# The chunk state of a state-space layer, held as 64x384 or as 128x192

## The chip, the cores and the metric

The kernel runs on one core of a Trainium2 chip. The metric is the device time of one execution in microseconds (us), the median of several runs. All data and all matrix products are in 32-bit floats.

## The reference

The kernel computes two residual layers on images of 64x64 positions with 192 channels, 8 of them. The change lies in layer 0, in its state-space part. For each image the 4096 positions are one sequence; a projection and a causal convolution give `x` (6 heads of 64 columns, 384 in all), `B` and `C` (64 columns each, shared by the heads), and a step `dt` for each head. With `A` negative for each head, the part that matters is:

```python
dA_cs = jnp.cumsum(dt * A, axis=2)                       # within a chunk
scores = einsum('bcin,bcjn->bcij', Cm, Bm)[..., None] * exp(seg) * dt   # masked: j <= i
y = einsum('bcijh,bcjhp->bcihp', scores, x)              # inside a chunk
decay_last = exp(dA_cs[:, :, -1:, :] - dA_cs)
states = einsum('bcjn,bcjh,bcjhp->bchnp', Bm, dt * decay_last, x)
chunk_decay = exp(dA_cs[:, :, -1, :])
new = carry * chunk_decay + states                       # from chunk to chunk
y = y + einsum('bcin,bchnp,bcih->bcihp', Cm, prev, exp(dA_cs))
```

So a chunk has a **state** of 64 numbers (`n`) for each of 384 columns (6 heads of 64). The **update** decays the state by one factor for each head and adds a product of the chunk's `B` and weighted `x`. The **readout** multiplies the state before the chunk with the chunk's `C` and scales each row by a factor for each head. The kernel works with chunks of 128 positions, which gives the same result as the reference's 256.

## The kernel before

**Stages.** `tile_kernel` runs `layer0` over all 8 images, and then `layer1`, which is four times as long and has nothing to do with the change. `layer0` cuts each image into 8 tiles of 512 positions (64 tiles, numbered `T`), and each tile into 4 chunks of 128 (256 chunks, numbered `c` within a tile).

**Order of the work.** `layer0` is written as 18 generators, among them `convolve`, `steps_in_time`, `scores`, `turn`, `states`, `mixer` and `output`. Each yields steps, and a step names an engine and a cost in us. A planner (`Flow`) plays these steps through as the program is built: it always issues the step that can start first by the written costs, with a small bonus from the generator's rank, and `keep` pins the order so found for each engine. On the chip each engine runs its queue in this order, and an instruction that has to wait holds up all behind it. `take` and `give` count the free buffers of a kind in the plan; `wait` waits for a mark that another generator sets.

**Buffers.** PSUM, which TensorE (PE) writes, has eight banks. Five have the tag `mm` and serve the wide products. Three have the tag `sm`, and everything that belongs to a chunk shares them: `p_g` (the product of `B` and `C`), `p_t` (the chunk's `x`, turned), `p_b` (its `B`, turned), `p_i` (readout), `p_n` (update), `p_y` (result inside the chunk), `p_u` (result turned back), and once a tile `p_c` (cumulative sums). `xdt`, `xw` and `t1` have one buffer each.

**Around the change.** `convolve` (L478 on) leaves `B` and `C` of a tile in one tile `cvb` of 128 partitions, 64 each, and two ACT instructions (L529, L530) put them through SiLU into `bm` and `cm`, each on partitions 0 to 63. `turn` turns `x` and `B` of a chunk (L715, L731); VectorE (DVE) makes of `p_t` the two weighted forms `xdt` (L721) and `xw` (L726). `dec` (L618) holds for each tile the factors for each chunk and head, in three planes: plane 1 is the factor of a row for the readout, plane 2 that of the whole chunk, the same on all 128 partitions. `states` then goes through the chunks:

- the readout: PE multiplies `cm` with the state `st`, both on 64 partitions, into `p_i` (L756), and DVE scales it into `t1` (L758); the first chunk of an image has none
- the update: PE multiplies `bt` and `xw` into 64 partitions of `p_n` (L767); DVE decays the old state (L777) and adds `p_n` (L780), both on 64 partitions by 384 columns. The first chunk of an image is a copy (L772).

`mixer` makes `p_y` from `e` and `xdt` (L803, L806), and DVE adds `t1` to it (L819). It holds its bank while it waits for `t1`.

On PE a product of f32 is issued as two passes, each with a weight load of its own (PEld), so that 256 products show as 512 matmuls.

Of the kernel before, what the change touches and what calls it, by code (L numbers as in the profile page):

```python
# [205 lines left out]
def layer0(tc, consts, x, x1s, mv1, w_in, w_out, w_fc1, w_fc2, rows):  # L206
# [12 lines left out]
    with ExitStack() as ctx:  # L219
# [260 lines left out]
        def convolve():  # L480

            for T, (b, t) in enumerate(tiles):
                yield "wait", ("cin", T, 0)
                cin = got["cin", T]
                yield "take", "cv"
                cv = got["cv", T] = tp.tile([128, 3, TT], F32, name="cv", bufs=2)
                cb = tp.tile([128, TT], F32, name="cvb")
                bm = got["bm", T] = tp.tile([NS, TT], F32, name="bm", bufs=2)
                cm = got["cm", T] = tp.tile([NS, TT], F32, name="cm", bufs=2)
                dst = [cv[:, 0], cv[:, 1], cv[:, 2], cb]  # L490
                done = [0.0] * 4
                for pair in ((0, 1), (2, 3)):
                    for mt in pair:
                        yield "wait", ("cin", T, mt)
                        done[mt] = yield step(
                            "ACT",
                            0.81,
                            lambda: [
                                nc.scalar.activation(
                                    dst[mt],  # L500
                                    cin[:, mt, 0:TT],
                                    AF.Identity,
                                    bias=v128["c1b"][:, mt : mt + 1],
                                    scale=c1w[:, mt, 0:1],
                                )
                            ],
                        )
                    for k in range(1, 4):
                        for mt in pair:
                            done[mt] = yield step(  # L510
                                "DVE",
                                0.77,
                                lambda: [
                                    nc.vector.scalar_tensor_tensor(
                                        dst[mt],
                                        cin[:, mt, k : k + TT],
                                        c1w[:, mt, k : k + 1],
                                        dst[mt],
                                        ALU.mult,
                                        ALU.add,  # L520
                                    )
                                ],
                                done[mt],
                            )
                cin_done(T, max(done))
                if t == NT - 1:
                    cin_done(T, max(done))
                yield step("ACT", 1.5, lambda: [nc.scalar.activation(cv, cv, AF.Silu)], max(done), "silu")
                yield step("ACT", 0.62, lambda: [nc.scalar.activation(bm, cb[0:64], AF.Silu)], None, "silu")  # L529
                f.at["cv", T] = yield step("ACT", 0.62, lambda: [nc.scalar.activation(cm, cb[64:128], AF.Silu)], None, "silu")  # L530

        def gate():
# [144 lines left out]
        def scores():  # L677

            for T in range(len(tiles)):
                yield "wait", ("cv", T)  # L680
                bm, cm = got["bm", T], got["cm", T]
                for c in range(NQ):
                    tk = slice(c * Q, c * Q + Q)
                    yield "take", "sm"
                    pg = qp.tile([128, DIN], F32, name="p_g", tag="sm")
                    q = yield step(
                        "PE",
                        0.26,
                        lambda: [nc.tensor.matmul(pg[:, :Q], bm[:, tk], cm[:, tk], start=True, stop=True)],
                        f.at["cv", T],  # L690
                    )
                    gm = ch.tile([128, Q], F32, name="gm")
                    q = yield step("DVE", 0.28, lambda: [nc.vector.tensor_mul(gm, pg[:, :Q], up)], q)
                    f.give("sm", q)
                    yield "wait", ("p", T, c)
                    e = got["e", T, c]
                    f.at["e", T, c] = yield step(
                        "DVE", 1.02, lambda: [nc.vector.tensor_mul(e, e, bc(gm, 1, [128, NH, Q]))]
                    )

        def turn():

            for T in range(len(tiles)):
                yield "wait", ("w2", T)
                yield "wait", ("cv", T)
                dt, w2, cv, bm = got["dt", T], got["w2", T], got["cv", T], got["bm", T]
                for c in range(NQ):
                    tk = slice(c * Q, c * Q + Q)
                    yield "take", "sm"
                    px = qp.tile([128, DIN], F32, name="p_t", tag="sm")  # L710
                    r = yield step(
                        "PE",
                        0.4,
                        lambda: [
                            nc.tensor.transpose(px[:, i * 128 : i * 128 + 128], cv[:, i, tk], ident) for i in range(3)  # L715
                        ],
                    )
                    yield "take", "xdt"
                    xdt = got["xdt", T, c] = ch.tile([128, DIN], F32, name="xdt", bufs=1)
                    f.at["xdt", T, c] = yield step(  # L720
                        "DVE", 0.55, lambda: [nc.vector.tensor_mul(hv(xdt), hv(px), bc(dt[:, c], 2, heads))], r  # L721
                    )
                    yield "take", "xw"
                    xw = got["xw", T, c] = ch.tile([128, DIN], F32, name="xw", bufs=1)
                    r = yield step(
                        "DVE", 0.55, lambda: [nc.vector.tensor_mul(hv(xw), hv(px), bc(w2[:, c], 2, heads))], r  # L726
                    )
                    f.give("sm", r)
                    yield "take", "sm"
                    pb = qp.tile([128, DIN], F32, name="p_b", tag="sm")  # L730
                    q = yield step("PE", 0.2, lambda: [nc.tensor.transpose(pb[:, :NS], bm[:, tk], ident[:NS, :NS])], 0.0)  # L731
                    f.fork(keep_b(T, c, pb, q, r))

        def keep_b(T, c, pb, q, r):
# [5 lines left out]
        def states():  # L740

            st = None
            for T, (b, t) in enumerate(tiles):
                yield "wait", ("w2", T)
                yield "wait", ("cv", T)
                dec, cm = got["dec", T], got["cm", T]
                if t == 0:
                    st = None
                for c in range(NQ):
                    tk = slice(c * Q, c * Q + Q)  # L750
                    if st is not None:
                        yield "take", "t1"
                        t1 = got["t1", T, c] = ch.tile([128, DIN], F32, name="t1", bufs=1)
                        yield "take", "sm"
                        pi = qp.tile([128, DIN], F32, name="p_i", tag="sm")
                        q = yield step("PE", 0.7, lambda: [nc.tensor.matmul(pi, cm[:, tk], st, start=True, stop=True)])  # L756
                        q = yield step(
                            "DVE", 0.55, lambda: [nc.vector.tensor_mul(hv(t1), hv(pi), bc(dec[:, 1, c], 2, heads))]  # L758
                        )
                        f.give("sm", q)  # L760
                        f.at["t1", T, c] = q
                    yield "wait", ("xw", T, c)
                    bt, xw = got.pop(("bt", T, c)), got.pop(("xw", T, c))
                    yield "take", "sm"
                    pn = qp.tile([128, DIN], F32, name="p_n", tag="sm")
                    q = yield step(
                        "PE", 0.7, lambda: [nc.tensor.matmul(pn[:NS], bt, xw, start=True, stop=True)], f.at["xw", T, c]  # L767
                    )
                    f.give("xw", q)
                    new = sp.tile([NS, DIN], F32, name="st")  # L770
                    if st is None:
                        q = yield step("DVE", 0.5, lambda: [nc.vector.tensor_copy(new, pn[:NS])], q)  # L772
                    else:
                        yield step(
                            "DVE",
                            0.6,
                            lambda: [nc.vector.tensor_mul(hv(new), hv(st), bc(dec[:NS, 2, c], 2, [NS, NH, HD]))],  # L777
                            0.0,
                        )
                        q = yield step("DVE", 0.55, lambda: [nc.vector.tensor_add(new, new, pn[:NS])], q)  # L780
                    f.give("sm", q)
                    st = new
                f.at["states", T] = q
# [1298 lines left out]
```

## Time and profile before

| what | us |
|---|---|
| median of 3 runs (lowest, highest) | 22789.71 (22783.53, 22798.81) |
| the profiled execution, its own time | 22798.87 |
| its span, first to last instruction | 22797.2 |
| PE busy over the span | 21475.4 (94%) |
| DVE busy | 21149.8 (93%) |
| ACT busy | 19859.8 (87%) |
| POOL busy | 16101.6 (71%) |
| stretch of layer 0 (100 to 4660 us of the span): PE, DVE, ACT, POOL busy | 4247.9, 3745.9, 3016.1, 611.5 |

The profile is of one execution. A busy time is the time in which an engine had an instruction under way; PE's is not PE at its peak, since matmuls are pipelined and their ends are modelled. A group of instructions is named by its line in the kernel, its engine and operation, and the tiles that it writes and reads; "idle before" is the time that the engine stood still just ahead of such instructions, with what ended it.

### The profile page before, as it was taken

The numbers are of one execution on the slowest core, as the hardware profiler recorded it, in microseconds if no ns is written. First come the engines' busy times: TensorE is split into PE (matmuls) and PEld (weight loads), VectorE is DVE, ScalarE is ACT, GpSimd is POOL, SyncE is SP. The second block draws the span as 40 slices with busy tenths as digits, with TensorE's granted clock in tenths as the row PEclk, the third lists the DMA queues.
The fourth block names the chain that finished last, engine by engine and source line by source line (L and its number), as shares of the span: only waits on it lengthen the run. The fifth ranks groups of instructions, "written<-read, shape, count | busy, mean of one in ns | idle before, by whom it ended". The sixth has DMA issues, their size and how long they took to land. (4 is left out here: it accounts for less than half of the span.)

```text
span 22797.2 us, 348200 instructions
## 1 busy us (share of the span) xinstructions
PE 21475.4 (94%) x118788; PEld 10903.6 (48%) x118788; DVE 21149.8 (93%) x22445; ACT 19859.8 (87%) x35227; POOL 16101.6 (71%) x12872
## 2 busy tenths in 40 slices
PE   8999999979999999999999999999999999999999
PEld 4444444435554555455545554554455445544554
DVE  7888888869999999999989998999899999999998
ACT  5666666759998999899989998999899989988998
POOL 1111111129995999599959995999599969987997
PEclk8999999989999999999999999999999999999999
DMA  2111111123333333333333333333333333333332
GB/s 53 44 42 46 46 44 46 41 85 93 93 93 109 91 94 94 110 92 93 93 109 93 93 91 110 92 95 92 110 93 94 89 114 93 93 84 116 93 94 78
DMA packets 1706714, 1954.31 MB, mean 86 GB/s; under 512 B 538112, under 2 KB 1039776, under 8 KB 1695712
## 3 DMA queue, kind: packets, MB, share of 16 engines
q1 hardware_dynamic: 1704928, 1932.03, 31.2%
q8 instruction: 933, 15.29, 0.3%
q14 instruction: 853, 6.99, 0.1%
HBM read 1316.16 MB, written 212.60 MB: 67 GB/s over the span
## 5 line engine op out<-in xcount | busy, mean ns | idle before, releaser
L1805 POOL TENSOR_TENSOR hs<-hs,cb 128x1024 f32<-128x1024 f32 x6144 | 14578.3, 2373 | 497.2 <-POOL cy L1803 4.0
L1791 DVE TENSOR_TENSOR_SCAN hs<-ea,cy,g 128x512 f32<-128x512 f32 x10752 | 12922.4, 1269 | 185.8 <-PE g L1775 170.1
L1749 ACT ACTIVATE ea<-dr,an 128x512 f32<-128x512 f32 x12288 | 8141.0, 710 | 454.7 <-DVE hs L1791 414.8
L1740 ACT ACTIVATE pw<-duT,bt 128x384 f32<-128x384 f32 x14304 | 7817.3, 601 | 19.4 <-DMA xo<-xt 19.4
L1820 PE MATMUL y<-hs,sel 128*64 128x512 f32 x24576 | 6629.7, 618 | 357.5 <-POOL hs L1805 337.3
L1775 PE MATMUL g<-ident,pw 128*128 128x128 f32 x43008 | 6101.0, 281 | 63.7 <-DVE hs L1791 15.5
L1775 PEld LDWEIGHTS g<-ident,pw 128*128 128x128 f32 x43008 | 4615.8, 141 | 2550.0 <-issue 1235.9
L1763 PEld LDWEIGHTS g<-dg,duT 128*64 128x64 f32 x24576 | 1556.6, 136 | 2067.5 <-issue 1497.9
L1803 POOL COPY cy<-hs 128x2 f32<-128x2 f32 x6144 | 1152.1, 188 | 1921.3 <-DVE hs L1791 1887.5
L1763 PE MATMUL g<-dg,duT 128*64 128x128 f32 x24576 | 2257.5, 282 | 182.0 <-DVE hs L1791 106.2
L1820 PEld LDWEIGHTS y<-hs,sel 128*64 128x64 f32 x24576 | 1234.0, 135 | 1560.2 <-issue 869.9
L1791 DVE TENSOR_TENSOR_SCAN hs<-ea,g 128x512 f32<-128x512 f32 x1536 | 1754.4, 1205 | 156.0 <-PE g L1775 122.0
L382 POOL TENSOR_TENSOR s<-xs 96x512 f32<-96x512 f32 x64 | 121.7, 1901 | 2138.7 <-DVE xs L360 1849.4
L1259 DVE SCALAR_TENSOR_TENSOR xs<-pad,p,xs 128x2048 f32<-128x2048 f32 x384 | 899.9, 2351 | 133.6 <-ACT xs L1243 123.7
L1654 PE MATMUL p_dt<-xdbl,wd 13*128 13x512 f32 x1536 | 869.7, 647 | 97.2 <-DVE duT L1683 71.5
L382 POOL TENSOR_TENSOR s<-sq 96x512 f32<-96x512 f32 x128 | 182.1, 1423 | 934.1 <-ACT sq L395 829.9
L1619 PE MATMUL p_d<-xc,wx 128*44 128x512 f32 x1536 | 797.0, 603 | 25.1 <-DMA xc<-xo 25.1
L972 PE MATMUL p_f<-h,wf 96*128 96x512 f32 x1536 | 756.5, 631 | 43.8 <-ACT zs L567 27.4
L360 DVE SCALAR_TENSOR_TENSOR x<-xx,p,x 96x512 f32<-96x512 f32 x1024 | 782.8, 814 | 15.2 <-ACT x L349 15.0
L360 DVE SCALAR_TENSOR_TENSOR xs<-xin,p,xs 96x512 f32<-96x512 f32 x1024 | 747.5, 771 | 3.7 <-ACT xs L349 3.7
L992 PE MATMUL p_f<-m,wf 128*96 128x512 f32 x1536 | 692.7, 601 | 0.0
L1676 PEld LDWEIGHTS p_du<-ident,de 128*128 128x128 f32 x3072 | 323.7, 141 | 617.7 <-DVE de L1667 407.1
(214 smaller groups left out, 19356.8 us busy)
## 6 DMA issues: line engine op xcount, KB each, us to landing
cb<-cd SPq DMA_DIRECT2D x4096, 128.0 KB
dr<-de SPq DMA_DIRECT2D x3072, 128.0 KB
xc<-xo SPq DMA_DIRECT2D x256, 768.0 KB
dg<-dz SPq DMA_DIRECT2D x256, 512.0 KB
e<-csd SPq DMA_DIRECT2D x256, 384.0 KB
ut<-xo SPq DMA_DIRECT2D x128, 768.0 KB
ut<-xo SPq DMA_DIRECT2D x256, 384.0 KB
xo<-xs SPq DMA_DIRECT2D x48, 1024.0 KB
```

The source lines that it names most:

```text
L360: nc.vector.scalar_tensor_tensor(im(out[:, ct]), tap(ct, j), w[:, ct, j : j + 1], im(out[:, ct]), ALU.mult, ALU.add)
L1259: nc.vector.scalar_tensor_tensor(xs, tap(d, h, j), kw[:, d, j : j + 1], xs, ALU.mult, ALU.add)
L1619: nc.tensor.matmul(st["p_d"][:44], wx[:, d, k], st["xc"][:, d], start=d == 0, stop=d == DT - 1)
L1654: nc.tensor.matmul(ps, st["wd"][32:45, d * 128 : d * 128 + 128], xds[s % 2][32:45], start=True, stop=True)
L1740: o(nc.scalar.activation(to, what, AF.Copy, scale=by))
L1749: nc.scalar.activation(ea[:, f], state[s]["dr", d][:, f], AF.Exp, scale=an[:, k, p, at : at + 1])
L1763: nc.tensor.matmul(gs[f][i * 64 : i * 64 + 64, j * 128 : j * 128 + 128], state[s]["duT"][:, j, (2 * d + f) * 64 : (2 * d + f) * 64 + 64], ...
L1775: nc.tensor.transpose(gs[f][:, j * 128 : j * 128 + 128], state[s]["pw", p, j][:, 2 * d + f].rearrange("p a b -> p (a b)"), ident,)
L1791: nc.vector.tensor_tensor_scan(rev(h[:, f]), rev(ea[:, f]), rev(g[f]), 0.0 if first(s) else state[s - 1]["cy"][:, p, d, f : f + 1], ALU.mu ...
L1803: o(nc.gpsimd.tensor_copy(st["cy"][:, p, d], h[:, :, last]))
L1805: o(nc.gpsimd.tensor_mul(h, h, bc(st["cb", p], 1, [128, 2, TT])))
L1820: o(nc.tensor.matmul(y[half[f]], sel, hc[:, f], start=p == ORDER[0] and k > 0, stop=p == ORDER[-1]))
```

## The change

The state becomes a tile of 128 partitions by 192 columns: heads 0 to 2 on partitions 0 to 63, heads 3 to 5 on partitions 64 to 127.

- The update's product is split in two products of 192 columns, which write partitions 0 to 63 and 64 to 127 of one `p_n`: they use different column groups of the array. DVE's decay, addition and copy then have 128 partitions by 192 columns.
- The readout is split in two products, which read the state's two halves and so use different row groups. Each writes a `p_i` of its own on 128 partitions, so the readout takes two `sm` banks, and two DVE instructions of 192 columns scale them into the two halves of `t1`.
- The second product needs `C` on partitions 64 to 127. `bm` becomes a SiLU of the whole of `cvb`, on 128 partitions: its upper half is `C`. The users of `B` read `bm[:NS]`.
- The decay needs the chunk factors of heads 0 to 2 on the lower half and of heads 3 to 5 on the upper half. Two POOL copies a tile bring them together in a new tile `keep`, of 128 partitions by 4 chunks by 3 heads.
- The costs that the planner is given change with it; the ranks stay.

```diff
@@ -485,7 +485,7 @@
                 yield "take", "cv"
                 cv = got["cv", T] = tp.tile([128, 3, TT], F32, name="cv", bufs=2)
                 cb = tp.tile([128, TT], F32, name="cvb")
-                bm = got["bm", T] = tp.tile([NS, TT], F32, name="bm", bufs=2)
+                bm = got["bm", T] = tp.tile([128, TT], F32, name="bm", bufs=2)
                 cm = got["cm", T] = tp.tile([NS, TT], F32, name="cm", bufs=2)
                 dst = [cv[:, 0], cv[:, 1], cv[:, 2], cb]
                 done = [0.0] * 4
@@ -526,7 +526,7 @@
                 if t == NT - 1:
                     cin_done(T, max(done))
                 yield step("ACT", 1.5, lambda: [nc.scalar.activation(cv, cv, AF.Silu)], max(done), "silu")
-                yield step("ACT", 0.62, lambda: [nc.scalar.activation(bm, cb[0:64], AF.Silu)], None, "silu")
+                yield step("ACT", 0.62, lambda: [nc.scalar.activation(bm, cb, AF.Silu)], None, "silu")
                 f.at["cv", T] = yield step("ACT", 0.62, lambda: [nc.scalar.activation(cm, cb[64:128], AF.Silu)], None, "silu")
 
         def gate():
@@ -686,7 +686,7 @@
                     q = yield step(
                         "PE",
                         0.26,
-                        lambda: [nc.tensor.matmul(pg[:, :Q], bm[:, tk], cm[:, tk], start=True, stop=True)],
+                        lambda: [nc.tensor.matmul(pg[:, :Q], bm[:NS, tk], cm[:, tk], start=True, stop=True)],
                         f.at["cv", T],
                     )
                     gm = ch.tile([128, Q], F32, name="gm")
@@ -728,7 +728,7 @@
                     f.give("sm", r)
                     yield "take", "sm"
                     pb = qp.tile([128, DIN], F32, name="p_b", tag="sm")
-                    q = yield step("PE", 0.2, lambda: [nc.tensor.transpose(pb[:, :NS], bm[:, tk], ident[:NS, :NS])], 0.0)
+                    q = yield step("PE", 0.2, lambda: [nc.tensor.transpose(pb[:, :NS], bm[:NS, tk], ident[:NS, :NS])], 0.0)
                     f.fork(keep_b(T, c, pb, q, r))
 
         def keep_b(T, c, pb, q, r):
@@ -740,44 +740,83 @@
         def states():
 
             st = None
+            HH = NH // 2
+            HC = HH * HD
+            half = [slice(i * NS, i * NS + NS) for i in range(2)]
+            cols = [slice(i * HC, i * HC + HC) for i in range(2)]
+            v3 = lambda ap: ap.rearrange("p (h d) -> p h d", h=HH)
             for T, (b, t) in enumerate(tiles):
                 yield "wait", ("w2", T)
                 yield "wait", ("cv", T)
-                dec, cm = got["dec", T], got["cm", T]
+                dec = got["dec", T]
+                queries = [got["cm", T], got["bm", T][NS:]]
                 if t == 0:
                     st = None
+                keep = sp.tile([128, NQ, HH], F32, name="keep")
+                yield step(
+                    "POOL",
+                    0.5,
+                    lambda: [
+                        nc.gpsimd.tensor_copy(keep[half[i]], dec[half[i], 2, :, i * HH : i * HH + HH]) for i in range(2)
+                    ],
+                )
                 for c in range(NQ):
                     tk = slice(c * Q, c * Q + Q)
                     if st is not None:
                         yield "take", "t1"
                         t1 = got["t1", T, c] = ch.tile([128, DIN], F32, name="t1", bufs=1)
-                        yield "take", "sm"
-                        pi = qp.tile([128, DIN], F32, name="p_i", tag="sm")
-                        q = yield step("PE", 0.7, lambda: [nc.tensor.matmul(pi, cm[:, tk], st, start=True, stop=True)])
+                        pi = []
+                        for i in range(2):
+                            yield "take", "sm"
+                            pi.append(qp.tile([128, DIN], F32, name="p_i", tag="sm"))
                         q = yield step(
-                            "DVE", 0.55, lambda: [nc.vector.tensor_mul(hv(t1), hv(pi), bc(dec[:, 1, c], 2, heads))]
-                        )
-                        f.give("sm", q)
+                            "PE",
+                            0.5,
+                            lambda: [
+                                nc.tensor.matmul(pi[i][:, :HC], queries[i][:, tk], st[half[i]], start=True, stop=True)
+                                for i in range(2)
+                            ],
+                        )
+                        for i in range(2):
+                            q = yield step(
+                                "DVE",
+                                0.33,
+                                lambda: [
+                                    nc.vector.tensor_mul(
+                                        v3(t1[:, cols[i]]),
+                                        v3(pi[i][:, :HC]),
+                                        bc(dec[:, 1, c, i * HH : i * HH + HH], 2, [128, HH, HD]),
+                                    )
+                                ],
+                                q,
+                            )
+                            f.give("sm", q)
                         f.at["t1", T, c] = q
                     yield "wait", ("xw", T, c)
                     bt, xw = got.pop(("bt", T, c)), got.pop(("xw", T, c))
                     yield "take", "sm"
                     pn = qp.tile([128, DIN], F32, name="p_n", tag="sm")
                     q = yield step(
-                        "PE", 0.7, lambda: [nc.tensor.matmul(pn[:NS], bt, xw, start=True, stop=True)], f.at["xw", T, c]
+                        "PE",
+                        0.5,
+                        lambda: [
+                            nc.tensor.matmul(pn[half[i], :HC], bt, xw[:, cols[i]], start=True, stop=True)
+                            for i in range(2)
+                        ],
+                        f.at["xw", T, c],
                     )
                     f.give("xw", q)
-                    new = sp.tile([NS, DIN], F32, name="st")
+                    new = sp.tile([128, HC], F32, name="st")
                     if st is None:
-                        q = yield step("DVE", 0.5, lambda: [nc.vector.tensor_copy(new, pn[:NS])], q)
+                        q = yield step("DVE", 0.3, lambda: [nc.vector.tensor_copy(new, pn[:, :HC])], q)
                     else:
                         yield step(
                             "DVE",
-                            0.6,
-                            lambda: [nc.vector.tensor_mul(hv(new), hv(st), bc(dec[:NS, 2, c], 2, [NS, NH, HD]))],
+                            0.35,
+                            lambda: [nc.vector.tensor_mul(v3(new), v3(st), bc(keep[:, c], 2, [128, HH, HD]))],
                             0.0,
                         )
-                        q = yield step("DVE", 0.55, lambda: [nc.vector.tensor_add(new, new, pn[:NS])], q)
+                        q = yield step("DVE", 0.33, lambda: [nc.vector.tensor_add(new, new, pn[:, :HC])], q)
                     f.give("sm", q)
                     st = new
                 f.at["states", T] = q
```

## The prediction

> **What bounds the kernel now.** I first read the slices of the span, to find the stretch that the change touches.
>
> ```profile
> PE   8999999979999999999999999999999999999999
> ...
> DVE  7888888869999999999989998999899999999998
> ...
> POOL 1111111129995999599959995999599969987997
> ```
>
> The first eight slices (570 us each), with POOL at one tenth, are layer 0; the `states` lines first and last start at 106 and 4659 us. The other 18.1 ms are layer 1, which the change doesn't touch. So I asked for the busy times of 100 to 4660 us alone:
>
> ```profile
> core 0: us, PE busy (x) PEld busy (x) DVE busy (x) ACT busy (x) POOL busy (x), PEclk, DMA share, GB/s
> 100.00:4660.00 4560.00, 4247.91 (x14463) 2106.78 (x14462) 3745.91 (x6259) 3016.09 (x5967) 611.46 (x505) 0.93 0.16 44
> ```
>
> PE is idle 4560 - 4248 = 312 us, DVE 814 us; ACT and POOL have room. No engine is full: two in-order queues wait for one another. The view of waits, DVE only, same stretch (total us, times, longest):
>
> ```profile
> DVE xdt L721 <- PE p_y L806: 350.3, 136, 9.6
> DVE xx L899 <- PE p_o L889: 113.2, 57, 5.7
> DVE gm L693 <- PE p_g L689: 86.1, 84, 3.3
> DVE st L780 <- PE p_n L767: 57.5, 70, 3.1
> DVE t L758 <- PE p_i L756: 49.7, 41, 5.8
> ```
>
> These five are 657 of DVE's 814 idle us, and all wait for PE. So PE is the slower partner, DVE a near second. To weigh a microsecond of each: for 814 us PE (or what it waits for) alone decides, for 312 us DVE or ACT alone; I split the other 3434 us evenly. PE's share is (814 + 1717)/4560 = 0.55, DVE's at most (312 + 1717)/4560 = 0.45. The even split is my choice.
>
> The instructions concerned, from the groups by line (xcount | busy us, mean ns | idle before):
>
> ```profile
> L767 PE MATMUL p_n<-xw,bt 128*64 128x384 f32 x512 | 242.3, 558 | 22.5 <-DVE yt L819 13.1 <-ACT yc L875 4.6 <-DVE gm L693 2.2
> L756 PE MATMUL p_i<-st,cm 64*128 64x384 f32 x496 | 241.1, 568 | 18.6 <-DVE yt L819 7.6 <-DVE st L780 3.3 <-ACT bt L736 2.8
> ...
> L777 DVE TENSOR_TENSOR st<-st,dec 64x384 f32<-64x384 f32 x248 | 144.4, 582 | 0.0
> ...
> L758 DVE TENSOR_TENSOR t<-p_i,dec 128x384 f32<-128x384 f32 x248 | 135.8, 548 | 50.8 <-PE p_i L756 49.7
> ...
> L780 DVE TENSOR_TENSOR st<-st,p_n 64x384 f32<-64x384 f32 x248 | 134.6, 543 | 63.4 <-PE p_n L767 57.5
> ...
> L693 DVE TENSOR_TENSOR gm<-p_g,up 128x128 f32<-128x128 f32 x256 | 72.1, 282 | 87.2 <-PE p_g L689 86.3
> ```
>
> Each f32 matmul appears as two (512 for 256 chunks). The two state matmuls use half of the array each, and DVE works on 64 of its 128 partitions at L777 and L780.
>
> **What the skill says.** The Trainium skill, "TensorE: Matmul & The Clock Gate", Part 3 (Packing small matmuls): matmuls on different row or column groups run at the same time, starting some 4 ns apart. For column groups this trace agrees, in layer 1 (start us, us):
>
> ```profile
> 10011.87 1.08 PE L1820 MATMUL y<-hs,sel 128*64 128x512 f32 x4
> ```
>
> Four 512-column matmuls, two into each half of the output, take 1.08 us; in layer 0 a run of twelve unpaired ones (2001.11, L992) takes 5.31 us, 0.44 each, so four would take 1.77. No pair of row groups occurs in this trace. "TensorEngine Tiling (Array Packing)", Gotcha 1 (PSUM Pressure): row tiles must write to different PSUM banks. That is why the readout now takes two `p_i`; the trace can't show it. "VectorE: DVE Perf Modes", perf-mode tier table: f32 tensor_tensor has only the one-element-per-cycle mode, so its time follows the elements in a partition. The trace agrees: L693 at 128 columns takes 282 ns, L758 at 384 takes 548, so 266/256 = 1.04 ns a column.
>
> **The change, part by part.**
>
> *Update on PE.* One product of 384 columns becomes two of 192 on two column groups. In a stream a 512-column matmul takes 0.43 us from start to start (L992), 0.84 ns a column. If the two overlap, each of a product's two passes drops 192 x 0.84 = 0.161 us: 0.322 us x 256 = 82 us. If they ran one after the other: 0, with four weight loads more to hide.
>
> *Readout on PE.* The same sum on row groups: 0.322 x 248 = 80 us. From below 0 (no overlap); below that, an exposed weight load (186 ns median) for each of 496 extra matmul passes would cost 92 us. I take the overlap, on the page's word.
>
> *DVE.* 192 columns fewer are 0.199 us less. L777 and L780: -0.199 x 248 each, -49.4 twice; L772: -0.199 x 8 = -1.6. L758 becomes two instructions of 548 - 199 = 349 ns in place of one of 548: +0.150 x 248 = +37. Sum -63 us. L777's mean of 582 lies above its minimum of 487, so part of it is not column work; if that shrank too the sum is some -75, if its start-up delay stays -63.
>
> *PE and DVE together.* 162 x 0.55 + 63 x 0.45 = 89 + 28 = 117 us. All of it on the path would be 225 us, a bound.
>
> *PSUM banks.* Seven names share three `sm` banks: `p_g`, `p_t`, `p_b`, `p_i`, `p_n`, `p_y`, `p_u`, and `p_c` once a tile. Summing first matmul to last reader over the trace's records gives 6090 us, 44.5% of 3 x 4560; `p_t` is held 7.6 us on average, `p_i` 2.8. A second `p_i` adds 2.8 x 248 = 690 us: 49.5%. A bank not yet read out stops PE's whole queue. PE's waits at an `sm` matmul for a DVE or ACT reader of such banks sum to 170 us today; rows like these:
>
> ```profile
> PE p_g L689 <- DVE t L758: 17.3, 6, 3.9
> PE p_b L731 <- DVE xw L726: 16.6, 23, 1.2
> PE p_n L767 <- DVE yt L819: 13.1, 12, 1.6
> ```
>
> Eight takes for seven, on fuller banks, and one that needs two at once: I estimate a quarter more, 42 us. From below 0, if the planner finds other work; from above see the second rival.
>
> *The copies to `keep`.* Two on POOL for each tile, 128 in all. POOL COPY of 128x2 at L1803 takes 188 ns, of 128x12 at L453 537: 24 to 69 us on an engine idle for 3949. Cost taken: 0, hidden there and behind the readout. If the cover is gone, the tile's first L777 waits behind one POOL sum (L940, 2.54 us), and with it all of DVE and the readers of its results: at most 64 x 2.54 = 163 us. A gain is excluded, as it only adds work. In the plan, the first readout of a tile comes 1.2 us later.
>
> *At nothing.* `bm` on 128 partitions: L529 takes 619 ns on 64 and has 512 columns either way. No DMA is added or moved; SP and its queue keep theirs. `xw` and `bt` come free a little earlier with the shorter update.
>
> *Re-planning.* The planner orders all of layer 0 by the written costs, so changed costs move much unrelated work, and the ranks were not changed with them. No row prices that; I take 0 and allow 40 us both ways.
>
> **Sum.** -117 + 42 = -75 us. The profiled execution's own time is 22798.9 us (span 22797.2, 1.7 around it), 9 above the median of 22789.7. So 22724 against its own time, 22715 against the median, which I predict.
>
> **Rivals.** *First: row groups don't overlap, or the plan eats half.* 82 x 0.55 + 28 - 42 = -31 us: 22759, within 0.2% (46 us, about what a measurement here can tell from no change). For it: no row pair in the trace. Against: column pairs overlap fully.
>
> *Second, slower: readouts starve the `sm` banks.* With each bank taken 44.5% of the time and independent, all three are taken 9% of the time, but at least two 42%. A third of 248 readouts, 82, would wait for one more bank, or make the next product wait. The mean hold is 6090/1830 takes = 3.3 us, with a long tail (`p_t`); the rest of one caught in the middle is about 2.5 us: 205 us on PE. Less the 117 gained, +88: 22878. It decides from 117/248 = 0.47 us of new wait for each readout. For it: `p_y` is held while `mixer` waits for `t1`, `p_t` while `turn` waits for `xdt` and `xw`, and both depend on `states`, which now needs the third and second bank. Against: the planner knows the slots, and the banks are half empty.
>
> *Third, it doesn't do what it says:* neither pair overlaps. 28 - 42 = +14 us: 22804, no difference.
>
> **How the numbers follow.** Likeliest case 0.62 (own range 22630 to 22744); first and third rival 0.2 together; second 0.18. Faster 0.62, same 0.20, slower 0.18. The range reaches from 22590 (200 less, nearly all of both savings on the path) to 22850, which takes in the first and third and the lighter half of the second.
>
> **What would show it.** L767's and L756's successors should show four matmuls of 192 columns for each chunk, paired within tens of ns, PE busy for each falling from 242 and 241 to near 130 us; DVE for `st` from 144 and 135 to near 95 and 85, `t` up from 136 to near 173. Layer 0 should end some 75 us sooner with layer 1 unchanged. Bank trouble would show as longer waits of PE at `p_i`, `p_n`, `p_b`, `p_g` for readers of `p_t`, `p_y`, `t`, and of DVE at `xdt` for `p_y` (350 us now). I am wrong if PE time of `p_i` stays, if these waits grow by over 100 us, or if layer 1 moves.

## The result and the profile after

The changed kernel takes 22826.3 us (median of 16 runs, 22810.3 to 22852.4), the kernel before, run beside it, 22790.4. The ratio is 1.0017, with a 95% interval of 1.0009 to 1.0025: by this ratio, which is used throughout, 39 us slower (the two medians differ by 36), where 75 us faster was forecast. The profiled execution took 22810.3 us, the quickest of the 16, so its trace shows somewhat less of the loss.

Layer 1 didn't move: from the last store of layer 0 to the end of the span it is 17993 us before and 17996 after. All that follows is about layer 0. First the stretch of 100 to 4660 us, with the same columns as before:

```profile
100.00:4660.00 4560.00, 4204.39 (x15430) 2188.05 (x15430) 3683.02 (x6489) 3009.97 (x5964) 677.92 (x631) 0.91 0.16 44
```

PE's and DVE's busy times went down, by 44 and 63 us (162 and 63 were forecast), and so did the granted clock, from 0.93 to 0.91. The groups by line say that the parts themselves came out as meant:

```profile
L785 DVE TENSOR_TENSOR t<-p_i,dec 128x192 f32<-128x192 f32 x496 | 168.6, 346 | 48.4 <-PE p_i L776 47.2 <-PE p_b L731 1.1
L776 PE MATMUL p_i<-st,bm 64*128 64x192 f32 x496 | 162.0, 410 | 11.8 <-DVE yt L858 9.1 <-ACT yc L914 1.6 <-DVE gm L693 0.8
...
L776 PE MATMUL p_i<-st,cm 64*128 64x192 f32 x496 | 160.4, 407 | 11.4 <-DVE yt L858 4.1 <-DVE xw L726 3.0 <-ACT yc L914 2.8
L803 PE MATMUL p_n<-xw,bt 128*64 128x192 f32 x1024 | 158.1, 391 | 29.9 <-DVE t L785 8.2 <-ACT yc L914 7.8 <-DVE gm L693 7.2
...
L816 DVE TENSOR_TENSOR st<-st,keep 128x192 f32<-128x192 f32 x248 | 90.5, 365 | 0.0
L819 DVE TENSOR_TENSOR st<-st,p_n 128x192 f32<-128x192 f32 x248 | 86.4, 348 | 57.2 <-PE p_n L803 51.2
```

DVE's decay and addition fell from 144.4 and 134.6 us to 90.5 and 86.4, and the two scalings rose from 135.8 to 168.6. PE's `p_n` fell from 242 to 158 us. The two halves of a readout lie on top of one another, so 162 and 160 are nearly the same time, where 241 was. Here is one readout in the timeline of PE (start us, us):

```profile
2054.09 0.43 PE L776 MATMUL p_i<-st,cm 64*128 64x192 f32 x1
2054.09 0.43 PE L776 MATMUL p_i<-st,bm 64*128 64x192 f32 x1
2054.35 0.32 PE L776 MATMUL p_i<-st,cm 64*128 64x192 f32 x1
2054.36 0.32 PE L776 MATMUL p_i<-st,bm 64*128 64x192 f32 x1
2054.61 0.60 PE L842 MATMUL p_y<-dsk,cv 128*128 128x128 f32 x3
```

The row groups run in pairs, 7 ns apart, and 0.53 us after the first start the next product begins. Before the change it was 0.84. But the waits of DVE, in the same stretch, are no shorter:

```profile
DVE xdt L721 <- PE p_y L845: 380.6, 157, 6.7
DVE xx L938 <- PE p_o L928: 97.7, 76, 4.0
DVE gm L693 <- PE p_g L689: 77.7, 81, 4.3
DVE st L819 <- PE p_n L803: 51.2, 63, 4.0
DVE t L785 <- PE p_i L776: 47.2, 42, 4.4
```

They sum to 654 us, as before (657). The work was saved, and PE's results came no earlier. To see where PE's time went I took, from the trace's records, the time from each product's start to the next one's, by product. `p_n` fell by 95 us, but `p_i` by 6 only (231 to 225), though one readout is 0.31 us shorter; `p_y` rose by 58, `p_f` of the first dense layer by 52, `p_u` by 22. Three things can do this: the order (the planner was given other costs), the second bank, and the clock. The records of the clock, which know full clock and half clock only, show PE at half of its clock for 669 us in layer 0 before, and for 922 after (the expectations below, which counted a little beyond layer 0, say 689 and 942). There a 512-column matmul takes 0.853 us to the next start, at full clock 0.429, so half clock costs at most half of the time that it lasts.

### The profile page after: what moved, and what is told of

It reads as the page before. It is cut to its first block, busy times and chain, and to the rows that moved or that the text cites. A ratio compares the mean times of both kernels' runs of the same rounds, so it can differ in the third digit from the quotient of the medians.

```text
span 22808.6 us, 350610 instructions
## 1 busy us (share of the span) xinstructions
PE 21440.0 (94%) x119796; PEld 10987.2 (48%) x119796; DVE 21096.1 (92%) x22693; ACT 19854.6 (87%) x35227; POOL 16168.4 (71%) x13000
## 5 line engine op out<-in xcount | busy, mean ns | idle before, releaser
L382 POOL TENSOR_TENSOR s<-x 96x512 f32<-96x512 f32 x64 | 92.5, 1446 | 777.2 <-DVE x L360 612.7
```

## The experiments

Each ratio is against the kernel before, run on the same chip. Differences between kernels are differences of ratios times 22790; where they set apart two measured ratios, both intervals enter, so that a step carries some 25 to 50 us either way. Each time at half clock, and each time from one product's start to the next one's, is of the profiled execution, to the end of layer 0.

**Order, banks or clock: four kernels.** First, the change with its products issued twice:

```diff
     nc.tensor.matmul(pi[i][:, :HC], queries[i][:, tk], st[half[i]], start=True, stop=True)
+    for _ in range(2)
     for i in range(2)
...
     nc.tensor.matmul(pn[half[i], :HC], bt, xw[:, cols[i]], start=True, stop=True)
+    for _ in range(2)
     for i in range(2)
```

> The changed kernel with every state product issued twice into the same place (update and readout), in the same order and with the same written costs. PE's work for the states is then as before the change (0.64 us a product in place of 0.32), all else as after. Theory A (the packing is worth what was forecast, and the new order with its second bank costs as much): the 162 us of PE work put back lengthen layer 0 by 0.55 of that, 89 us: about 22915. Theory B (PE, made less busy, is granted its full clock less often, and the PE saving is given back there): the granted clock of layer 0 rises from 0.91 towards the 0.93 of before, time at half clock falls from 942 us towards 700, and the time stays within 25 us of the changed kernel's 22826.

Measured: 1.0048 (1.0036 to 1.0061), 22897 us; 71 us above the change. Theory B alone falls. It isn't empty: PE's time on the two products grew by 156 us, the other products' fell by 71, and the time at half clock fell from 922 to 795. Of the 71 us, 27 are less idle time of PE (439 to 411); the 127 us of half clock are at most 64 us of lost work. So a saving on PE comes back in part as waiting, and in part, it seems, through the clock.

Second, the change without its packing:

```diff
-    nc.tensor.matmul(pi[i][:, :HC], queries[i][:, tk], st[half[i]], start=True, stop=True)
+    nc.tensor.matmul(pi[i][:, :HC], queries[0][:, tk], st[:, cols[i]], start=True, stop=True)
...
-    nc.tensor.matmul(pn[half[i], :HC], bt, xw[:, cols[i]], start=True, stop=True) for i in range(2)
+    nc.tensor.matmul(pn[:NS], bt, xw, start=True, stop=True)
...
-    nc.vector.tensor_mul(v3(new), v3(st), bc(keep[:, c], 2, [128, HH, HD]))
+    nc.vector.tensor_mul(hv(new), hv(st), bc(dec[:NS, 2, c], 2, [NS, NH, HD]))
...
-    nc.vector.tensor_add(new, new, pn[:, :HC])
+    nc.vector.tensor_add(new, new, pn[:NS])
```

> The changed kernel's order, costs, copies, two banks for a readout and two scalings of 192 columns, but the state kept as 64x384: one update product of 384 columns, two readout products of 192 from the same 64 rows (which can't run at once), decay and addition on 64x384. So it is the change without its packing. Theory A: order and banks cost some 150 us and the packing saves 117: about 22940. Theory B: order and banks cost little: before plus 0.45 of the 37 us that the two scalings add, 22790 to 22830, at a granted clock near 0.93 in layer 0.

Measured: 1.0084 (1.0070 to 1.0098), 22976 us. Theory A, and more of it: order, banks and the second scaling cost 191 us, where the prediction had 59 (42 for the bank, 17 for the scaling). The packing then brings back 150: about 82 by DVE's part (from here to the kernel with doubled products, whose PE load is nearly the same) and 71 by PE's. The forecast had 134 for both, 45 and 89. So against the same work unpacked in the same order, the packing is worth about what was forecast.

Third, only the update packed, with the costs, takes and steps of before, and so in its order. `cz` holds C on one half of the partitions and zeros on the other, once either way, so that one bank takes both products; the copies to `keep` are issued in an older step:

```diff
-    nc.tensor.matmul(pi, cm[:, tk], st, start=True, stop=True)
+    nc.tensor.matmul(pi[:, cols[i]], cz[:, i, tk], st, start=True, stop=True) for i in range(2)
...
-    nc.tensor.matmul(pn[:NS], bt, xw, start=True, stop=True)
+    nc.tensor.matmul(pn[half[i], :HC], bt, xw[:, cols[i]], start=True, stop=True) for i in range(2)
...
-    nc.vector.tensor_mul(hv(new), hv(st), bc(dec[:NS, 2, c], 2, [NS, NH, HD]))
+    nc.vector.tensor_mul(v3(new), v3(st), bc(keep[:, c], 2, [128, HH, HD]))
...
-    nc.vector.tensor_add(new, new, pn[:NS])
+    nc.vector.tensor_add(new, new, pn[:, :HC])
```

> The kernel before with its own order, costs and one bank for a readout, and only the update packed: state 128x192, two update products of 192 columns on column groups, decay and addition on 128x192. The readout multiplies with C padded by zeros on the other half (two unpaired products of 192 columns on all rows, same PE time as before) into one bank; one more ACT instruction and two POOL copies a tile. Expected PE -82 us, DVE -97 us of work. Theory A (the order was at fault): 82 x 0.55 + 97 x 0.45 = 89 us less than before, about 22700. Theory B (the clock gives PE's part back): only DVE's 44 us remain, about 22745, and time at half clock rises above the 689 us of before.

Measured: 0.9935 (0.9922 to 0.9949), 22642 us: 148 faster, better than either theory. The readout of this kernel isn't quite that of before, as it runs on all 128 rows, and ACT has one instruction more in each tile; the readout's share is told apart below. PE's products stand in the order of before, in all 14320 records.

Fourth, the same work in another order:

```diff
-        f.LAG, f.STAY, f.RANK = 0.684, -0.464, -0.01
+        f.LAG, f.STAY, f.RANK = 0.7, -0.464, -0.01
```

> The kernel before with one planner constant moved (LAG 0.684 to 0.70), so that the same work is ordered differently. Theory A (an order drawn afresh is worse than the one that the constants were chosen for): 40 to 150 us slower, 22830 to 22940. Theory B: within 25 us of 22790.

Measured: 0.9953 (0.9940 to 0.9965): 107 us **faster**. Both theories were wrong on this: the order is worth 100 us, and the given one was not the best. The 40 us that the prediction allowed for re-planning were too few.

**Is it a bad draw of the order, or the second bank?** The change with the same edit:

```diff
-        f.LAG, f.STAY, f.RANK = 0.684, -0.464, -0.01
+        f.LAG, f.STAY, f.RANK = 0.7, -0.464, -0.01
```

> The changed kernel with the planner constant LAG moved from 0.684 to 0.70, as was done to the kernel before (which gained 107 us by it). Theory O (the order is a matter of luck; the changed kernel drew a bad one, and the second bank matters little): another draw is better, by some 100 us as for the kernel before: about 22720. Theory K (a readout that needs two of three banks at once makes every order worse): it stays at 22790 to 22870, well above the 22683 that the kernel before has at this LAG.

Measured: 0.9954 (0.9939 to 0.9968). At this LAG the change and the kernel before are level. A better order helped both by some 100 to 140 us, and the change brings nothing in either. So it isn't one unlucky draw, as theory O had it, and theory K's floor of 22790 fell too.

The change with its plan and order, but one bank really used:

```diff
-    pi = []
-    for i in range(2):
-        yield "take", "sm"
-        pi.append(qp.tile([128, DIN], F32, name="p_i", tag="sm"))
+    yield "take", "sm"
+    yield "take", "sm"
+    pi = qp.tile([128, DIN], F32, name="p_i", tag="sm")
...
-    nc.tensor.matmul(pi[i][:, :HC], queries[i][:, tk], st[half[i]], start=True, stop=True)
+    nc.tensor.matmul(pi[:, cols[i]], cz[:, i, tk], st, start=True, stop=True)
```

> The changed kernel in its own order (the plan still takes two banks), but the readout really uses one: C padded by zeros, two unpaired products of 192 columns into one bank, still two scalings; one more ACT instruction a tile. Against the changed kernel it gives up the readout's packing, half of the 71 us that issuing both products twice cost: +35, so 22860 if waits for the second bank on the chip cost nothing (theory O, and K if the bank works through the plan alone). If waits for the bank on the chip are what costs (K on the chip), it falls by what they cost, below 22810.

Measured: 0.9967 (0.9954 to 0.9980), 114 us below the change, with the readout's packing given up. So what the readout got costs more than it saves.

The packed update of the third kernel in another order:

```diff
-        f.LAG, f.STAY, f.RANK = 0.684, -0.464, -0.01
+        f.LAG, f.STAY, f.RANK = 0.7, -0.464, -0.01
```

> The kernel before with only the update packed (22642 at LAG 0.684), at LAG 0.70. If order and work add up, the kernel before's gain of 107 at this LAG comes on top: about 22535. If PE is the only limit left and the order of 0.684 suited this work, it stays between 22600 and 22680.

Measured: 0.9896 (0.9880 to 0.9913). Order and work nearly add up.

The kernel before, with a second `take` of `sm` in the plan alone and no second bank:

```diff
     yield "take", "sm"
+    yield "take", "sm"
     pi = qp.tile([128, DIN], F32, name="p_i", tag="sm")
...
     f.give("sm", q)
+    f.give("sm", q)
```

> The kernel before, unchanged in its work, but its plan counts two sm banks for each readout (one is used). It prices the second bank as the planner sees it. Theory K: fewer choices for the planner, 50 to 150 us slower, 22840 to 22940. Theory O: a new draw of the order, within 110 us of 22790 on either side.

Measured: 1.0008 (0.9999 to 1.0017), 18 us, which its interval can't tell from none. So theory K's 50 to 150 us are out: in the plan, at this LAG, the second bank costs little.

**Bank or row groups?** The one-bank kernel with its two products, still on all rows, in two banks:

```diff
-    yield "take", "sm"
-    yield "take", "sm"
-    pi = qp.tile([128, DIN], F32, name="p_i", tag="sm")
+    pi = []
+    for i in range(2):
+        yield "take", "sm"
+        pi.append(qp.tile([128, DIN], F32, name="p_i", tag="sm"))
...
-    nc.tensor.matmul(pi[:, cols[i]], cz[:, i, tk], st, start=True, stop=True)
+    nc.tensor.matmul(pi[i][:, :HC], cz[:, i, tk], st, start=True, stop=True)
```

> The one-bank kernel of the changed order (22727, or 0.9967 of before) with one thing put back: its two readout products, still of C padded by zeros on all 128 rows, go into two banks as in the change. Theory K (waiting for the second bank on the chip costs the 0.5% that lies between that kernel and the change): back to about 1.002 of before, 22830. Theory M (the row groups themselves cost it: products on 64 rows need a change of the array's mode, 0.093 us on either side, or count less for the clock): it stays at 0.9967, 22720.

Measured: 0.9990 (0.9982 to 0.9998), 22768 us: half way. The second bank costs 0.0023, 52 us, and the row groups, against the same two products on all rows, 0.0027, 62 us, though the change has one ACT instruction a tile fewer than this kernel. Both theories hold in half.

The one-bank kernel again, in another order:

```diff
-        f.LAG, f.STAY, f.RANK = 0.684, -0.464, -0.01
+        f.LAG, f.STAY, f.RANK = 0.7, -0.464, -0.01
```

> The one-bank kernel of the changed order at LAG 0.70, where the changed kernel stands at 0.9954 of before. If the second bank (or the row groups) cost as much in another order, this is 0.5% below that: 0.9904, 22580. If the cost was a matter of the one order, it is 0.9954 again, 22695.

Measured: 0.9924 (0.9909 to 0.9939), 68 us below the change at the same LAG: the cost is there in the second order too, somewhat smaller.

**The mode of the array.** The kernel before, its readout on all rows and nothing else; the upper 64 partitions of `cz` and of the two state tiles `sts` are zero:

```diff
-    nc.tensor.matmul(pi, cm[:, tk], st, start=True, stop=True)
+    nc.tensor.matmul(pi, cz[:, tk], sts[(T * NQ + c + 1) % 2], start=True, stop=True)
```

> The kernel before, in its own order, with one edit: the readout's product of 384 columns runs on all 128 rows of the array (C and the state padded by zeros on the upper 64 partitions) in place of 64. Nothing else is changed; no packing, one bank. Theory R (a product on 64 rows costs a change of the array's mode on both sides, 0.093 us each, and helps the granted clock less): PE saves 0.19 us x 248 = 46 us or some more, the time at half clock falls below 669 us, and the kernel is 25 to 45 us faster: 22745 to 22765. Theory N (the row groups cost nothing; what the two-bank kernel on full rows gained over the change has another cause): 22790, no difference.

Measured: 0.9966 (0.9954 to 0.9979): 77 us faster, for more multiplications, all of them by zero. The timeline of PE shows where it saves. First the kernel before, then this one:

```profile
2038.55 1.02 PE L889 MATMUL p_o<-yc,wo 128*96 128x512 f32 x2
2039.50 0.91 PE L756 MATMUL p_i<-st,cm 64*128 64x384 f32 x2
2040.34 1.10 PE L889 MATMUL p_o<-yc,wo 128*96 128x512 f32 x2
```

```profile
2005.94 3.70 PE L467 MATMUL p_x<-h,wi 96*128 96x512 f32 x8
2009.48 0.81 PE L759 MATMUL p_i<-stz,cz 128*128 128x384 f32 x2
2010.13 1.88 PE L467 MATMUL p_x<-h,wi 96*128 96x512 f32 x4
```

From the readout's start to the next product it is 0.84 us on 64 rows and 0.65 on 128. Of the difference, 0.10 us lie between the readout's two passes (0.427 against 0.326) and 0.09 behind the second (0.413 against 0.322). Before the readout, the last 512-column product takes 0.522 us to the next start where the readout has 64 rows, and 0.429 where it has 128. The first pass of the product after it is longer too, by 0.08 us in the mean: the `p_o` above, with weights of 96 columns, takes 0.507, and 0.429 in the midst of a stream.

The weight loads (PEld) show where a part of this lies. First the kernel before, then this one:

```profile
2039.50 0.29 PEld L756 LDWEIGHTS p_i<-st,cm 64*128 64x128 f32 x2 [0.79 <-issue]
2040.34 0.24 PEld L889 LDWEIGHTS p_o<-yc,wo 128*96 128x96 f32 x2 [0.55 <-issue]
```

```profile
2009.06 0.19 PEld L759 LDWEIGHTS p_i<-stz,cz 128*128 128x128 f32 x1 [0.24 <-issue]
2009.48 0.19 PEld L759 LDWEIGHTS p_i<-stz,cz 128*128 128x128 f32 x1 [0.24 <-issue]
```

On 64 rows the readout's first load starts with its own product, at 2039.50, and so does the load of the next product, at 2040.34. On all rows it starts a product earlier, at 2009.06 for 2009.48. This holds through layer 0 of the kernel before: at its 629 changes from more than 64 rows to 64 and its 605 changes back, the load starts 2 ns before its matmul (median; 1 to 3 ns in the middle eight tenths), and between two products on more than 64 rows 182. So the load isn't hidden across such a border, and the first pass behind it is longer by more, the more columns the weights have: by 0.10 us with 128 (`p_f`, 0.533 against 0.432), by 0.08 with 96 (`p_o`). The 0.10 between the two passes of the readout, whose weights have 128 columns, is of this size too. The Trainium skill, "TensorEngine Tiling (Array Packing)", Key Properties, says that a change of the tiling mode drains the array. The 0.09 us on either side fit this, though no run takes the drain apart from the loads.

With this readout the changes to 64 rows fall from 629 to 450 and those back from 605 to 432, since some readouts stand beside another product on 64 rows. At 0.19 us for one change (0.093 and 0.10) and 0.17 for one back (0.09 and 0.08) that is an estimate of 64 us of PE's time. The time at half clock fell too, from 669 to 614.

So the last products on 64 rows were moved as well, in the packed-update kernel at LAG 0.70:

```diff
-    nc.scalar.activation(bm, cb[0:64], AF.Silu)
+    nc.scalar.activation(bm, cb, AF.Silu)
...
-    bm, cm = got["bm", T], got["cm", T]
+    bm, cm = got["bm", T], got["cz", T][:, 0]
...
-    nc.tensor.transpose(pb[:, :NS], bm[:, tk], ident[:NS, :NS])
+    nc.tensor.transpose(pb[:, :Q], bm[:, tk], ident)
```

> The fastest kernel so far (packed update, one-bank readout on full rows, LAG 0.70; 0.9896 of before, 22553) with the last two products on 64 rows moved to all 128 as well: the scores of B and C (B with C above it, times C with zeros below it) and the turn of B (turned together with C). Theory R: two changes of mode less for each, 0.19 us x 512 = 95 us less on PE, 15 us more for the wider turn; 0.55 of the 80 us, 44 or somewhat more: about 0.9876, 22508. Theory N: 0.9896 again.

Measured: 0.9849 (0.9836 to 0.9863), 22455 us, 348 below the kernel before and 107 below the kernel that it was made from, where 44 or somewhat more was expected. No product on 64 rows is left in the state-space part, and this kernel beats both; half-clock time in its layer 0 is 430 us.

## Why the prediction was wrong

**The step that failed is the re-planning**, which the prediction put at 0 with 40 us either way: with the second scaling, for which it had 17 us, it cost 73. The runs lead from the kernel before to the change in five steps:

| step | ratios | us | forecast |
|---|---|---|---|
| readout on all rows in place of 64 | 1 to 0.9966 | -77 | |
| update packed (PE 82, DVE 100 us of work by the forecast) | 0.9966 to 0.9935 | -71 | -90 |
| the change's plan and order, two scalings | 0.9935 to 0.9967 | +73 | +17 (DVE 37 x 0.45), order 0 |
| a real second bank | 0.9967 to 0.9990 | +52 | +42 |
| row groups in place of all rows | 0.9990 to 1.0017 | +62 | |
| first and last together: the readout's packing | | -15 | -44 |
| sum | 1 to 1.0017 | +39 | -75 |

The forecast missed by 114 us, of which the third row is 56. It alone lies clear of its forecast, with some 42 us either way. The others miss by 29 (the readout), 19 and 10, all within their intervals, so that these differences may be noise.

**Re-planning: the miss.** The order and the second scaling cost 73 us at LAG 0.684 and 64 at 0.70 (0.9924 against 0.9896), so it isn't one draw. 33 us of DVE work for the scalings are in it. With the state unpacked, the order, the bank and the scaling cost 191 us where 59 were forecast. One move of LAG is worth 89 to 143 us in four kernels, all to the same side, so that 40 us were too narrow as well. Of the plan's own edits only the second `take` was tried alone (18 us); what the new costs and the `keep` step do apart from each other stays open.

**What bounds it, and the weights.** The split of 0.55 and 0.45 is neither borne out nor refuted. In the order of the change 156 us of PE's time were worth 71, and DVE's part of the packing 82 where 45 was written, each with some 35 to 45 us either way. Which of the two engines weighs more stays open.

**Update: right in kind, near in size.** 0.79 us from start to next start became 0.48, the 0.31 forecast. 71 us of the 90 came.

**Readout: right on the overlap, blind to the borders.** I took 0.322 us for each readout "on the page's word" and the trace gives 0.31 (the first rival's row groups without overlap are out): the Trainium skill, "TensorE: Matmul & The Clock Gate", Part 3, was right on the overlap, though the pairs start 7 ns apart here and not 4. But one of my signs of being wrong came: PE's time of `p_i` stayed (231 and 225 us). I had looked for nothing at the borders of a 64-row product, though 0.093 us stood in the trace of before on one side of each: row groups keep that, and all rows are rid of it. Between two products on all rows, with what it costs its neighbours (0.09 us before it and 0.09 on the first pass after it), the packed readout takes 0.70 us, and the unpacked one on all rows 0.66. So over this simpler remedy the packing had nothing to win. With order and banks the same, the row groups are 62 us slower than all rows. PE is at half clock for 922 us there, against 778. At most half of the difference, 72 us, is lost work, so the clock is large enough to account for most of it. The same page of the Trainium skill (Part 1) says that the clock is granted by PE's recent activity, and the doubled products agree. Whether a product on 64 rows counts as less activity, or something else lowers the clock, these runs don't settle.

**Banks: near in size, by luck.** 42 us were forecast and 52 measured, but the 42 were a quarter more of PE's waits for readers of `sm` tiles, and these don't show it: they sum to 170 us before, 207 after, and 203 in the one-bank kernel of the same order. The trace's records do: what comes late on PE right after a readout (over 0.1 us beyond the median) sums to 18 us before, 57 after, 53 with two banks on all rows and 20 with one (outside half clock 5, 30, 29 and 12). The rest of the 52 may be the clock: 778 us at half clock with two banks on all rows, 700 with one. The second rival had this mechanism, at 205 us four times too dear.

**The copies to `keep`** were right: POOL's 128 copies take 63.6 us, and the idle time of DVE before L816 is 0.0.

## What to carry to other kernels

Before packing small products, look at what stands on both sides of one: the time to the next start, against the same product at full height. Here padding with zeros to all 128 rows cost wider tiles for `C` and for the state, and won more than row groups did, without a second bank. Where an order is planned from written costs, the effect of an edit is known only with the order held fixed, or over several orders; otherwise the order's own 100 us are taken for the edit's.

## What the runs showed of the hardware

- A product of f32 on 64 rows between products on all rows, with 384 columns: 0.84 us to the next start, 0.093 before it, and 0.08 on the first pass of the next product; on all rows 0.65, 0 and 0. The column-tiled update pays a border too: 0.522 us for the 512-column product ahead of it, where a stream has 0.429.
- Across such a border the weight load starts 2 ns before its matmul, while between products on more than 64 rows it starts 182 ns before (medians, layer 0 of the kernel before).
- Pairs keep something of a border inside: the second pass starts 0.267 us after the first on row groups and 0.213 on column groups, where 192 columns stream in 0.16. It is paid once: issued twice, the readout takes 0.85 us in place of 0.53 and the update 0.80 in place of 0.48, which is 0.16 for each further pass.
- The granted clock moved with PE's load: with 156 us of products issued twice, the other products took 71 us less, 27 of them idle time, and the time at half clock fell from 922 to 795 us.
